# Leaf tiles that gather their rows through a slot-to-token table, in place of rows scattered into block order

## The chip, the cores and the metric

The kernel runs on one core of a Trainium2 chip. A core has a matrix engine (TensorE, PE in the profile), a vector engine (VectorE, DVE), a scalar engine (ScalarE, ACT), GpSimd (POOL) and a sync engine (SyncE, SP) that issues transfers; 16 DMA engines carry them out. SP, ACT and POOL each have a queue from which they issue DMAs; an indirect DMA, whose rows are addressed by a table of indices in on-chip memory, is issued from POOL. The metric is the device time of one execution in microseconds (us); lower is better.

## The reference

The input is x, 4 sequences of 1024 tokens with 256 features. The result is a "macaron": half a feed-forward block, an attention, half a second feed-forward block, each on a layernorm of x:

```python
x = x + 0.5 * ffn(layernorm(x), weights)
x = x + attention(layernorm(x), ...)          # 16 heads, causal by pages of 64
x = x + 0.5 * ffn(layernorm(x), weights)      # the same weights
```

The feed-forward block is itself made of four hard-routed trees (q, k, v and f), each of depth 8 with 256 leaves, and a softmax attention over 256 features between them:

```python
def fff(x, nw, nb, w1, b1, w2, b2, act):
    node = 0
    for _ in range(8):
        node = 2 * node + 1 + (x . nw[node] + nb[node] > 0)
    leaf = node - 255
    return act(x @ w1[leaf] + b1[leaf]) @ w2[leaf] + b2[leaf]   # 256 -> 16 -> 256

xn = normalised x
q, k, v = fff(xn, q...), fff(xn, k...), fff(xn, v...)           # relu
y = xn + softmax(q k^T / 16) v
ffn = y + fff(y, f...)                                           # gelu
```

Every token thus goes to one of 256 leaves in each tree, and each leaf has its own two small weight matrices.

## The kernel before, in words

The 4096 tokens are 32 token tiles of 128 rows (NT). The 256 leaves of a tree are 32 blocks of 8 (NBLK). The top five levels of a tree choose the block; the last three levels are decided inside the block.

**Routing.** `routes` (L392) and `route` (L349) take four token tiles at a time: TensorE transposes rows, multiplies them with the top nodes and with a table of ancestors, and VectorE makes a one-hot of the block for each token (`oh`) and running counts per block (`acc`). For q, k and v one pass serves all three trees.

**Placement.** `place` (L511) gives each token a slot. Blocks come in order, and each block's run of slots is rounded up to whole tiles of 128, so a "leaf tile" holds tokens of one block alone; there are at most 63 leaf tiles (NGRP). `counts`, `tiles_of`, `ends_of` and `ranks` (L423 to L455) compute the slot as the block's first slot plus the token's rank in it, the rank by a product with a triangular matrix; `blocks_ended` and `tile_blocks` (L463, L499) compute which block each leaf tile belongs to (`gblk`, `sel`, `own`).

**Scatter.** `scatter` (L586) sends the normalised rows of one token tile from on-chip memory to a DRAM array `xs` at the slots: one indirect DMA on POOL a token tile, 32 a tree (L593). Slots that no token fills must hold harmless numbers, so the arrays are cleared once at the start (`clear`, L300), two of 8064 KB on SP's queue for q, k and v, and one for f on ACT's queue during the tree attention. In f's array each row has one more column, the token's number, and the padding holds 4096 there.

**Leaves.** `leaves` (L704) works through the leaf tiles in a software pipeline, one iteration a tile: `load` (L709) issues a plain 128 KB load of the tile's rows on SP, four tiles ahead (PRE); `turn` transposes it on TensorE (L718) and ACT evicts it (L720); `hidden` multiplies with the block's 8 first-layer matrices and the 7 lower nodes (L736), and VectorE makes the mask of the leaf taken (L752, L756, L759) and applies it (L766); `active` transposes the masked hidden values (L780) and the mask (L781), ACT applies the activation (L789), VectorE scales the transposed mask (mT, L791); `result` multiplies with the second-layer matrices (L797) and with b2 (L798). For q, k and v ACT evicts the result (L812) and SP stores it in slot order (`osrt`); for f VectorE adds the row (L802) and POOL scatters the rows back to their tokens (`ytok`, L803), leaving out those numbered 4096 or more. Tiles 0 to 47 always run; `spare_leaves` (L685) runs 48-52, 53-57 and 58-62 only where the count of used tiles asks for them.

**Between the trees.** `load_first` (L653) builds the first-layer weights of a tree: 64 transposes and 16 evictions of about 1 us (L675 on VectorE, L677 on ACT). `with_steps` (L1022) interleaves the leaf tiles of q (and of k) with the placement and the scatters of the next tree. During v's leaves, and in the tree attention, `fetch` (L836) gathers the q, k and v results back into token order by the slots (L842, one indirect DMA on POOL a token tile and tree).

**Head of the first block.** After the routing, `split_b2` (L273) loads the four b2, splits them into three bf16 parts (POOL, L288 and L290) and writes the parts by 56 plain DMAs on ACT's queue into DRAM images; then `load_b1` (L628) loads b1 and the lower nodes' offsets by 48 DMAs on ACT's queue and splits them on VectorE. Only then come the placement of q, its 32 scatters, and the rest of the weights' build.

**f.** The tree attention, a token tile a step, is written in program order on TensorE, VectorE, ACT and POOL (`in_order`, L130): what an engine is to do comes in exactly the order of the code. A plan (`at`, `due`) hangs small pieces on its 32 steps. f is routed there as soon as a tile's y is ready (`weigh`, L870), and placed in three runs (`in_runs`, L530), so that the scatters of the first 24 token tiles go out during steps 27 to 29, four more at step 30, and the last four after the last route, between the evictions of the weights' build (L1222-1247). The f leaf stage and the addition to the residual close the block.

## Time and profile before

| what | us |
|---|---|
| three runs, median (lowest to highest) | 2688.52 (2675.3 to 2690.43) |
| the profiled execution, its own time | 2682.69 |
| its span in the trace | 2680.8 |
| TensorE busy | 2214.2 (83%) |
| VectorE busy | 1440.4 (54%) |
| ScalarE busy | 1061.1 (40%) |
| GpSimd busy | 628.3 (23%) |
| first leaf tile turned (L718), first block | 185.4 |
| first leaf tile turned, second block | 1874.6 |
| q leaf stage, tiles 0 to 47, first and second block | 192.7 to 277.1, 1880.7 to 1963.4 |
| f leaf stage, tiles 0 to 47, first and second block | 868.0 to 943.5, 2558.0 to 2635.2 |

In a row of groups the profile gives the line, the engine, the operation, what it writes and reads, how often, its busy time and mean duration, and the idle time of the engine just ahead of it with what ended it. In a list of waits it gives the engine and line that waited, on which engine and line, how long in total, how often, and the longest. A window row gives the window's start and end, its length, and for each engine its busy time and number of instructions, then TensorE's granted clock (1.00 is full speed), the busy share of the DMA engines and their GB/s. The TensorE clock granted over the execution was 0.921.

### The profile page before, as it was taken

The numbers are of one execution on the slowest core, as the hardware profiler recorded it, in microseconds if no ns is written. First come the engines' busy times: TensorE is split into PE (matmuls) and PEld (weight loads), VectorE is DVE, ScalarE is ACT, GpSimd is POOL, SyncE is SP. The second block draws the span as 40 slices with busy tenths as digits, with TensorE's granted clock in tenths as the row PEclk, the third lists the DMA queues.
The fourth block names the chain that finished last, engine by engine and source line by source line (L and its number), as shares of the span: only waits on it lengthen the run. The fifth ranks groups of instructions, "written<-read, shape, count | busy, mean of one in ns | idle before, by whom it ended". The sixth has DMA issues, their size and how long they took to land. (4 is left out here: it accounts for less than half of the span.)

```text
span 2680.8 us, 42431 instructions
## 1 busy us (share of the span) xinstructions
PE 2214.2 (83%) x13989; PEld 1414.2 (53%) x13989; DVE 1440.4 (54%) x4870; ACT 1061.1 (40%) x2645; POOL 628.3 (23%) x752
## 2 busy tenths in 40 slices
PE   5038689899996979999999999972958899999684
PEld 2037568666664854443444434331747776666473
DVE  6046566433343876666666667743646553333375
ACT  4024345422223313555555555551434452222241
POOL 0244042322331621100101100004303222332243
PEclk9569899999998979999999999996989899999897
DMA  8676667423214420000000000015556662320434
GB/s 272 206 278 201 222 197 235 156 61 93 83 46 144 149 70 1 1 1 1 1 1 1 1 1 1 1 61 203 187 202 202 213 182 81 104 91 31 161 122 154
DMA packets 230592, 296.21 MB, mean 110 GB/s; under 512 B 25786, under 2 KB 208715, under 8 KB 226257
## 3 DMA queue, kind: packets, MB, share of 16 engines
q1 hardware_dynamic: 150704, 172.27, 19.7%
q0 software_dynamic: 26352, 67.20, 7.7%
q10 hardware_dynamic: 53296, 53.72, 6.3%
q8 instruction: 130, 2.13, 0.3%
q14 instruction: 110, 0.89, 0.1%
HBM read 165.97 MB, written 131.96 MB: 111 GB/s over the span
## 5 line engine op out<-in xcount | busy, mean ns | idle before, releaser
L1461 DVE TENSOR_REDUCE mxh<-big 128x1 f32<-128x512 f32 (+3 forms) x768 | 393.1, 552 | 193.8 <-PE big L1453 191.8
L1497 ACT ACTIVATE pTh<-big 128x512 f32<-128x512 f32 (+3 forms) x768 | 341.3, 491 | 289.1 <-PE big L1453 265.3
L1453 PE MATMUL big<-kTh,qTh 32*128 32x512 f32 (+3 forms) x1536 | 403.1, 540 | 1.5 <-ACT kTh L1434 1.4
L1489 PE MATMUL big<-qTh,kTh 32*128 32x512 f32 (+3 forms) x1536 | 399.8, 536 | 1.9 <-ACT pTh L1497 1.6
L720 ACT COPY xgT<-sm 128x256 f32<-128x256 f32 x399 | 148.9, 375 | 286.8 <-PE sm L718 141.1
L855 PE MATMUL two<-kT,qT 128*128 128x512 f32 x512 | 239.8, 613 | 10.2 <-issue 8.9
L883 PE MATMUL sm<-vb,pT 128*128 128x256 f32 x1024 | 238.2, 387 | 0.2 <-ACT pT L879 0.2
L1489 PEld LDWEIGHTS big<-qTh,kTh 32*128 32x128 f32 x1536 | 143.3, 184 | 156.7 <-issue 127.0
L718 PE MATMUL sm<-ident,xg 128*128 128x128 f32 x798 | 159.0, 283 | 76.2 <-DMA xg<-xs 73.1
L883 PEld LDWEIGHTS sm<-vb,pT 128*128 128x128 f32 x1024 | 193.8, 194 | 26.9 <-ACT pT L879 1.0
L863 DVE TENSOR_REDUCE mx<-two 128x1 f32<-128x1024 f32 x64 | 78.3, 1223 | 206.0 <-PE two L855 167.6
L1508 PE MATMUL sm<-pTh,vpad 128*32 128x512 f32 (+3 forms) x1536 | 165.4, 502 | 0.0
L1453 PEld LDWEIGHTS big<-kTh,qTh 32*128 32x128 f32 x1536 | 146.9, 185 | 20.4 <-issue 14.3
L855 PEld LDWEIGHTS two<-kT,qT 128*128 128x128 f32 x512 | 96.2, 198 | 111.0 <-issue 107.8
L752 DVE SCALAR_TENSOR_TENSOR went<-sm,sides 128x14 bf16<-128x14 f32 x399 | 66.9, 168 | 152.6 <-PE sm L743 77.5
L780 PE MATMUL sm<-ident,hm 128*128 128x128 f32 x399 | 113.9, 285 | 39.2 <-DVE hm L766 29.0
L812 ACT COPY og<-sm 128x256 f32<-128x256 f32 x298 | 111.1, 373 | 74.5 <-ACT hid L789 30.4
L842 POOL DMA_INDIRECT y_q<-os_q,slot_q x64 | 60.4, 944 | 314.0 <-PE sm L1054 309.8
L718 PEld LDWEIGHTS sm<-ident,xg 128*128 128x128 f32 x798 | 85.7, 148 | 87.0 <-issue 66.5
L789 ACT ACTIVATE hid<-sm 128x128 f32<-128x128 f32 x399 | 112.6, 282 | 45.5 <-PE sm L781 34.1
L803 POOL DMA_INDIRECT ytok<-og,tok x101 | 99.4, 984 | 125.2 <-DVE four L756 94.9
L885 DVE SCALAR_TENSOR_TENSOR xn<-sm,rs,xn 128x256 f32<-128x256 f32 x64 | 31.0, 485 | 170.6 <-PE sm L883 118.7
(316 smaller groups left out, 4279.4 us busy)
## 6 DMA issues: line engine op xcount, KB each, us to landing
xg<-xs SPq DMA_DIRECT2D x298, 128.0 KB
xs<-zero SPq DMA_DIRECT2D x2, 8064.0 KB
xs_f<-zero ACTq DMA_DIRECT2D x14, 1028.0 KB
xg<-xs_f SPq DMA_DIRECT2D x101, 128.5 KB
os_q<-og SPq DMA_DIRECT2D x101, 128.0 KB
os_v<-og SPq DMA_DIRECT2D x101, 128.0 KB
os_k<-og SPq DMA_DIRECT2D x96, 128.0 KB
raw_q<-in_q_w SPq DMA_DIRECT2D x8, 1024.0 KB
```

Of the source, the lines that this page charges most:

```text
L718: nc.tensor.transpose(pa[:, c, :], xg[:, c * P : (c + 1) * P], ident)
L720: nc.scalar.copy(xT, pa)
L780: nc.tensor.transpose(pt[:, 0], hm, ident)
L789: nc.scalar.activation(hid, pt[:, 0], func)
L812: nc.scalar.copy(og, po)
L855: nc.tensor.matmul(ps[:, n0 : n0 + 512], qT[:, c, i * P : (i + 1) * P], kT[:, c, n0 : n0 + 512], start=(c == 0), stop=(c == KC - 1),)
L883: nc.tensor.matmul(po, pT[:, j, :], vb[:, j, :], start=(j == 0), stop=(j == TPB - 1))
L1453: matmul = nc.tensor.matmul(ps[:, :n], qT[r : r + HPAD, hg, i * P : (i + 1) * P], kT[r : r + HPAD, hg, n0 : n0 + n], start=True, stop=True,)
L1461: nc.vector.tensor_reduce(maxima(b, hg)[:, i, c, u : u + 1], ps[:, :n], AX.X, ALU.max)
L1489: matmul = nc.tensor.matmul(ps[:, off:], kT[r : r + HPAD, hg, j * P : (j + 1) * P], qT[r : r + HPAD, hg, qb * QN + off : (qb + 1) * QN], s ...
L1497: nc.scalar.activation(pT[:, u, off:], ps[:, off:], AF.Exp, scale=1.0 / math.sqrt(HD))
L1508: nc.tensor.matmul(acc[r : r + HPAD, off:], vpads[b % 2][:, j, 4 * hg + 2 * pair + u, :], pTs[pair][:, u, off:], start=(j == 0), stop=(j = ...
```

## The change

**No more row arrays in block order.** The scatters of rows, the clearing of their arrays, the extra token column and its cast are gone. In their place the normalised rows are kept in DRAM in token order, with 128 zero rows behind them (`rows`, `keep_rows`): for q, k and v by eight plain stores of 512 KB on ACT's queue during the routing, for f by one store of 128 KB on SP's queue per token tile. `leaves.load` becomes an indirect gather on POOL, whose indices are a column of a table `inv`: for each leaf tile the tokens in its 128 slots, and a number of at least 4096 where there is none. f scatters its results by the same table. The first 48 tiles of a tree also issue the gathers of the four tiles behind them.

**The table.** `placement` replaces `place`, `ranks` and `in_runs`. It takes eight token tiles at a time (for f pieces of 8, 8, 8, 4 and 4). `low` computes each token's rank in its block, how many whole tiles lie before it and its lane in the tile, and a one-hot of the lane. `high` adds the block's first tile and makes a one-hot of the leaf tile, multiplied once by the token tile's base less 4096 and once by the token's own partition number; products of the lane one-hot with these two sum up the table. For f, `low` of the first three pieces is hung on steps 12, 20 and 27, of the fourth on step 31; `low` of the last and all of `high` follow the last route, a step of weights' build between each.

**Other moves.** mT moves from VectorE to ACT. b2's loads go to SP's queue and its writes to POOL's, and `split_b2` is placed ahead of the routing; the loads of b1 go to SP's queue and its splitting from VectorE to POOL. The eight loads of x are issued together at the start. The weights' raw loads have two buffers for q, k and v where they had three.

```diff
-    xs = [dram.tile([NSLOT, E], F32, name=f"xs_{n}") for n in range(2)]
+    rows = [dram.tile([NTOK + P, E], F32, name=f"rows_{n}") for n in "xy"]
     osrt = [dram.tile([NSLOT, E], F32, name=f"os_{nm}") for nm in FFFS[:3]]
-
-    xs += [xs[0], dram.tile([NSLOT, E + 1], F32, name="xs_f")]
     ytok = dram.tile([NTOK, E], F32, name="ytok")
 
 
-    SPARE = (48, 53, 58, NGRP)
-
-
-    zero = const.tile([P, E + 1], F32, name="zero")
-    nc.vector.memset(zero[:, :E], 0.0)
-    nc.vector.tensor_scalar_add(zero[:, E:], pid, float(NTOK))
+    SPARE = (0, 48, 53, 58, NGRP)
+
+
+    zero = const.tile([P, E], F32, name="zero")
+    nc.vector.memset(zero, 0.0)
+    for r in rows:
+        nc.gpsimd.dma_start(r[NTOK:], zero)
...
-            nc.scalar.dma_start(
+            nc.sync.dma_start(
                 rest[f * NBLK : (f + 1) * NBLK].rearrange("p (q c) -> p q c", c=E),
                 a[f"{nm}_b2"].rearrange("(q p) c -> p q c", p=NBLK),
             )
             for lo in (0, B2W - E):
-                nc.scalar.dma_start(b2i[f][:, lo : lo + E], none[:B2R])
+                nc.gpsimd.dma_start(b2i[f][:, lo : lo + E], none[:B2R])
         for s in range(3):
             nc.gpsimd.tensor_copy(part[s], rest)
             if s < 2:
                 nc.gpsimd.tensor_sub(rest, rest, part[s])
-        for f in range(len(FFFS)):
-            for s in range(3):
+            for f in range(len(FFFS)):
                 for r in range(B2G):
                     p = s * NBLK + r * EPB
-                    nc.scalar.dma_start(
+                    nc.gpsimd.dma_start(
...
-    def row_of(f, t):
-        return xn[:, t, : E + (f == 3)]
+    def keep_rows(queue, f, lo, hi):
+        queue.dma_start(
+            rows[f // 3][lo * P : hi * P].rearrange("(i p) e -> p i e", p=P), xn[:, lo:hi, :]
...
+    def placement(pool, oh, acc, pieces, gblk, sel, own, inv, slot=None, ahead=False):
+
+
+
+        parts = {}
+
+        def part(nm, c, shape, dtype, bufs=2):
+            tag = f"{nm}{c}" if ahead else nm
+            return pool.tile(
+                shape, dtype, name=f"{nm}{c}", tag=tag, bufs=1 if ahead else bufs
+            )
+
+        def low(c):
+
+            lo, hi = pieces[c]
+            n, ts_ = hi - lo, slice(lo, hi)
+            pr = sm([P, n, NBLK])
+            nc.tensor.matmul(pr, tri, oh[:, ts_, :], start=True, stop=False)
+            nc.tensor.matmul(pr, ones, acc[:, ts_, :], start=False, stop=True)
+            row = pool.tile([P, n, NBLK], F32, name="row", tag="row")
+            nc.vector.tensor_tensor(row, pr, oh[:, ts_, :], ALU.mult)
             yield
...
+            rank = pool.tile([P, n], F32, name="rank", tag="rank")
+            nc.vector.tensor_reduce(rank, row, AX.X, ALU.add)
+            whole = 1.5 * 2.0**23
+            past = part("past", c, [P, n], F32)
+            nc.vector.tensor_scalar(past, rank, 1.0 / P, 0.5 / P - 0.5, ALU.mult, ALU.add)
+            nc.vector.tensor_scalar_add(past, past, whole)
+            nc.vector.tensor_scalar_add(past, past, -whole)
+            lane = part("lane", c, [P, n], F32)
+            nc.vector.scalar_tensor_tensor(lane, past, -float(P), rank, ALU.mult, ALU.add)
+            yield
+            in_lane = part("in_lane", c, [P, n, P], BF16, 1)
+            nc.vector.tensor_tensor(in_lane, bc(lanes, 1, n), bc(lane, 2, P), ALU.is_equal)
+            parts[c] = past, lane, in_lane
+            yield
+
+        def high(c, first, table):
+
+            lo, hi = pieces[c]
+            n, ts_ = hi - lo, slice(lo, hi)
+            past, lane, in_lane = parts.pop(c)
+            row = pool.tile([P, n, NBLK], F32, name="row", tag="row")
+            nc.vector.tensor_tensor(row, oh[:, ts_, :], bc(first, 1, n), ALU.mult)
+            at = pool.tile([P, n], F32, name="at", tag="at")
+            nc.vector.tensor_reduce(at, row, AX.X, ALU.add)
+            nc.vector.tensor_add(at, at, past)
+            if slot is not None:
+                nc.vector.scalar_tensor_tensor(
+                    slot[:, ts_], at, float(P), lane, ALU.mult, ALU.add
+                )
+            yield
+            tiles = pool.tile([P, n, GCOL], BF16, name="tiles", tag="tiles")
+            nc.vector.tensor_tensor(tiles, bc(numbers, 1, n), bc(at, 2, GCOL), ALU.is_equal)
+            both = pool.tile([P, n, 2, GCOL], BF16, name="both", tag="both", bufs=2 - ahead)
+            nc.scalar.activation(both[:, :, 1], tiles, AF.Copy, scale=pid)
+            yield
+            nc.vector.tensor_tensor(both[:, :, 0], tiles, bc(starts[:, ts_], 2, GCOL), ALU.mult)
+            pi = sm([P, 2, GCOL])
+            for i in range(n):
+                nc.tensor.matmul(
+                    pi, in_lane[:, i, :], both[:, i], start=(i == 0), stop=(i == n - 1)
+                )
+            yield
+            if c:
+                nc.vector.tensor_tensor(table, table, pi[:, 0], ALU.add)
+            else:
+                nc.vector.tensor_scalar_add(table, pi[:, 0], float(NTOK))
+            nc.vector.tensor_tensor(table, table, pi[:, 1], ALU.add)
+            yield
+
+        def rest(done=0):
+
+            ng = tiles_of(pool, counts(pool, acc, NT))
+            yield
+            end = ends_of(pool, "gend", ng, 0.0)
+            first = pool.tile([P, NBLK], F32, name="first", tag="first")
             nc.vector.tensor_sub(first, end, ng)
...
             yield
...
+            table = pool.tile([P, GCOL], F32, name="table", tag="table")
+            for c in range(len(pieces)):
+                if c >= done:
+                    yield from low(c)
+                yield from high(c, first, table)
+            nc.vector.tensor_copy(inv, table)
             found = []
...
+            yield from blocks_ended(pool, acc, found)
             yield
...
+            tile_blocks(pool, found[0], end, gblk, sel, own)
+
+        return low, rest
...
-        nc.vector.memset(b1[:, P + SUB :], 0.0)
+        nc.gpsimd.memset(b1[:, P + SUB :], 0.0)
         yield
-        nc.vector.tensor_copy(b1p[f], b1)
+        nc.gpsimd.tensor_copy(b1p[f], b1)
         for k in range(1, 3):
             for q in range(k, 3):
                 one = slice(q * NBLK, (q + 1) * NBLK)
-                nc.vector.tensor_sub(b1[one], b1[one], b1p[f][one])
-                nc.vector.tensor_copy(b1p[f][one], b1[one])
+                nc.gpsimd.tensor_sub(b1[one], b1[one], b1p[f][one])
+                nc.gpsimd.tensor_copy(b1p[f][one], b1[one])
...
         def load(g):
-            width = xs[f].shape[1]
-            xg = pool.tile([P, width], F32, name="xg", tag="xg", bufs=PRE + 3 * (1 + f // 3))
-            nc.sync.dma_start(xg, xs[f][g * P : (g + 1) * P, :])
+            if g < SPARE[1] + PRE:
+                xg = pool.tile([P, E], F32, name="xg", tag="xg", bufs=PRE + 3 * (1 + f // 3))
+            else:
+                xg = pool.tile([P, E], F32, name="xh", tag="xh", bufs=2 + 4 * (f // 3))
+            nc.gpsimd.indirect_dma_start(
+                out=xg,
+                out_offset=None,
+                in_=rows[f // 3],
+                in_offset=bass.IndirectOffsetOnAxis(ap=inv[:, g : g + 1], axis=0),
+            )
             return xg
...
-            nc.vector.tensor_scalar(mT, pt[:B2R, 1], own[:, g : g + 1], None, ALU.mult)
+            nc.scalar.activation(mT, pt[:B2R, 1], AF.Copy, scale=own[:, g : g + 1])
...
-                tok, xg = kept.pop(g)
-                nc.vector.tensor_tensor(og, po, xg[:, :E], ALU.add)
+                nc.vector.tensor_tensor(og, po, kept.pop(g), ALU.add)
                 nc.gpsimd.indirect_dma_start(
                     out=places[g],
-                    out_offset=bass.IndirectOffsetOnAxis(ap=tok, axis=0),
+                    out_offset=bass.IndirectOffsetOnAxis(ap=inv[:, g : g + 1], axis=0),
...
+        end = hi if part else hi + PRE
         for g in range(lo - PRE, hi + 5):
-            if g + PRE < hi:
-                rows[g + PRE] = load(g + PRE)
+            if g + PRE < end and g + PRE not in got:
+                got[g + PRE] = load(g + PRE)
...
+        keep_rows(nc.sync, 3, t, t + 1)
...
+                        if first:
+                            for t in range(0, NT, GT):
+                                nc.sync.dma_start(
+                                    xres[:, t : t + GT, :],
+                                    a["x"][
+                                        t // TPB, (t % TPB) * P : (t % TPB + GT) * P, :
+                                    ].rearrange("(i p) e -> p i e", p=P),
+                                )
+                            split_b2(stage(rt, "b2", 1))
...
+                            keep_rows(nc.scalar, 0, lo, lo + GT)
...
-                    drain(placing(0, None, slot[0]))
-                    drain(scattering(0, slot[0], None, NT))
-                    drain(build)
+                    drain(placing(0), build)
...
-                        ahead = load_raw(raw, f + 1, 3)
-                        rows = []
-                        with_steps(
-                            leaves(*what),
-                            placing(f + 1, rows),
-                            scattering(f + 1, slot[f + 1], rows, 1),
-                        )
+                        ahead = load_raw(raw, f + 1)
+                        with_steps(leaves(*what), placing(f + 1))
...
+                pieces = [(0, 8), (8, 16), (16, 24), (24, 28), (28, 32)]
+                low_f, rest_f = placement(
+                    pf, *hot_f, pieces, gblk[3], sel[3], own[3], inv[3], ahead=True
+                )
+                paths, lows = [], {}
...
+                for c, step in ((0, 12), (1, 20), (2, 27)):
+                    for i in range(3):
+                        at(step + i // 2, 1 + i % 2, place_low, c)
                 for where in range(3):
-                    at(31, where, place_run, 1, 1)
+                    at(31, where, place_low, 3)
...
-                    place_run(2, 1)
-                    drain(islice(build, 3))
-                    place_run(2, 1)
-                    go(*range(RUNS[2], NT))
-                    for _ in range(3):
-                        place_run(2, 1)
-                        drain(islice(build, 2))
+                    place_low(4)
+                    drain(islice(build, 2))
+                    place_low(4)
+                    place_low(4)
+                    for _ in rest_f(len(pieces)):
+                        drain(islice(build, 1))
                     drain(build)
```

## The prediction

> **What bounds the kernel now.** I read the page's totals first, then the windows by stage, the chain of waits, the groups of GpSimd (POOL), and last the timelines of the leaf stages.
>
> ```profile
> span 2680.8 us, 42431 instructions
> PE 2214.2 (83%) x13989; PEld 1414.2 (53%) x13989; DVE 1440.4 (54%) x4870; ACT 1061.1 (40%) x2645; POOL 628.3 (23%) x752
> ```
>
> TensorE bounds the whole, but 17% of the span is holes, and the change touches only these and the leaf stages. Windows (busy us and counts of PE, PEld, DVE, ACT, POOL; granted clock; DMA):
>
> ```profile
> 75.00:100.00 25.00, 2.03 (x6) 0.56 (x6) 0.46 (x3) 0.00 (x0) 3.30 (x2) 0.50 0.85 277
> 100.00:125.00 25.00, 0.00 (x0) 0.00 (x0) 0.00 (x0) 0.00 (x0) 11.28 (x7) 0.50 0.45 133
> 150.00:175.00 25.00, 3.65 (x16) 3.27 (x16) 4.24 (x4) 4.08 (x4) 18.90 (x21) 0.56 1.04 390
> 192.00:277.00 85.00, 75.73 (x561) 63.37 (x560) 57.71 (x284) 41.78 (x138) 30.66 (x32) 0.99 0.62 202
> 422.00:497.00 75.00, 73.70 (x596) 65.47 (x595) 52.98 (x233) 48.08 (x159) 19.84 (x21) 1.00 0.64 188
> 868.00:944.00 76.00, 72.18 (x545) 60.89 (x546) 68.01 (x324) 26.10 (x92) 44.35 (x46) 1.00 0.44 135
> 1830.00:1870.00 40.00, 4.83 (x41) 4.48 (x39) 6.50 (x7) 6.04 (x6) 25.96 (x28) 0.62 0.76 277
> ```
>
> Two heads are nearly empty: 75 to 185 us, and 1830 to 1870 us. The leaf stages of q (192-277), v (422-497) and f (868-944) each do 48 leaf tiles with TensorE 89 to 98% busy; in f VectorE is at 89% too. POOL has room everywhere: 0.26 to 0.58 of a stage. The waits name the first head:
>
> ```profile
> POOL b_part L288 <- DMA b2i_f<-b_none: 94.6, 1, 94.6
> DVE cnt L428 <- DMA b_f<-in_f_nb: 59.7, 1, 59.7
> PE sm L718 <- DMA xg<-xs: 73.1, 4, 37.9
> DVE xn L885 <- remote: 40.7, 6, 9.0
> ```
>
> The routing is done by 70 us; b2 then waits for its loads behind the clearing of the row arrays (2 x 8064 KB), and the split (97-111) and the writes of b2 and b1 on ScalarE's queue last until 133. Slots come at 141, 32 scatters run until 182, and the first leaf tile is turned (L718) at 185.4. The POOL groups (busy, mean ns | idle before):
>
> ```profile
> L593 POOL DMA_INDIRECT xs<-xn,slot_q x64 | 61.7, 964 | 85.7 <-DVE slot_q L454 66.8 <-issue 18.0 <-DMA xs<-xn,slot_q 0.6
> L842 POOL DMA_INDIRECT y_q<-os_q,slot_q x64 | 60.4, 944 | 314.0 <-PE sm L1054 309.8 <-issue 4.3
> L803 POOL DMA_INDIRECT ytok<-og,tok x101 | 99.4, 984 | 125.2 <-DVE four L756 94.9 <-DVE went L752 17.7 <-issue 6.2
> ```
>
> An indirect DMA costs POOL 0.94 to 0.98 us, scatter or gather, plus a gap. The timelines show the gap and a side effect (start, duration, [idle before <- releaser]):
>
> ```profile
> 535.69 0.95 POOL L842 DMA_INDIRECT vb<-os_v,slot_v  x1 [0.30 <-issue]
> 543.36 1.22 DVE L863 TENSOR_REDUCE mx<-two 128x1 f32<-128x1024 f32 x1 [9.54 <-remote]
> 228.62 0.96 POOL L593 DMA_INDIRECT xs<-xn,slot_k  x1 [0.30 <-issue]
> 229.95 0.96 POOL L593 DMA_INDIRECT xs<-xn,slot_k  x1 [0.36 <-issue]
> 231.70 0.37 ACT L720 COPY xgT<-sm 128x256 f32<-128x256 f32 x1 [1.88 <-PE sm L718]
> 873.51 0.98 POOL L803 DMA_INDIRECT ytok<-og,tok  x1 [0.55 <-DVE four L756]
> ```
>
> Back to back, one gather takes 1.25 us (0.95 + 0.30). After 17 such gathers (519-540) VectorE had stood for 9.5 us for a matmul long finished: completions of TensorE reach the others late while POOL issues without pause. In the q stage every third tile stalls 1.3 us after three scatters in a row (tile intervals 1.51, 1.51, 2.81). In f, one scatter per 1.54 us leaves gaps of 0.55 and nothing stalls. So a leaf stage is as fast as TensorE only while POOL pauses.
>
> **The change part by part**, against the profiled execution's own 2682.7 us (span 2680.8), which lies 5.8 below the median of 2688.5.
>
> **First head.** Clears and 32 scatters leave; b2 starts at once. POOL: loads in by about 25 us (5 MB of x and b2 at 246 GB/s, the first window's rate, from 3 us), three casts and two subtractions 3 x 1.89 + 2 x 4.05 = 14 us, 58 plain DMAs (8 `none`, 48 parts, 2 zero tails), then b1's copies, moved from VectorE, some 8 us. No row shows a plain DMA of POOL: ScalarE's queue took 0.35 to 0.9 us each for the same writes, an indirect one of POOL takes 1.25; I take 1.25 as the row of the same engine, 73 us. End: 25+14+73+8 = 120; the first gather (1.25) and its landing (2.1) give 123. The other end (0.35 each, 20 us) makes POOL free at 67; then the placement ends it: routing 70, four pieces of 5.3 us of VectorE (five 256-element operations at 0.42 us, one of 1024 at 1.2 and two of 512 at 0.68, as L863 and L879 have them, and four small ones at 0.15) with a hop through ScalarE and TensorE, about 30, so 104. First turn 123 for 185.4: **-62** (-81 to -45; the 48 b1 loads, now on SP's queue ahead of the weights, hide beside the routing). What is late next is w1: its 16 evictions of 1.06 us follow the placement in order, and L736 needs them two tiles after the turn.
>
> **Second head.** Slots at 1819.5-1826 and scatters until 1868 become a placement of about 29 us from 1819.5, then a gather: first turn 1857 for 1874.6, **-18** (-30 to -10).
>
> **q and k stages.** Scatters of the next tree, with their stalls, leave (1.78 to 1.58 us a tile, 47 intervals: -9.4), and 48 gathers spread at one per tile come: 0.95 of 1.58 us, so a pause of 0.63, as f has now. mT leaves VectorE (L791, 340 ns) for ScalarE, whose three evictions (375+282+373 = 1.03 us) become 1.3 of 1.55, hidden. The placement of the next tree (21 us of VectorE, 36 small matmuls of TensorE, 3 us) replaces ranks and 32 slot casts. **-9 x 4 = -36** (-44 to -16). Each of the four starts of k and v makes two to three gathers (1.25) ahead of its first tile, behind the spares: **+12** in all.
>
> **v stages.** POOL has 52 gathers and 24 fetches (L842) in each: 76 x 1.25 = 95 us for 75-77. Bare, +14 to +18 each; with no pause, late completions add a few: **+40** (+28 to +60). The fetches can't be hidden elsewhere: the gather of a tile is queued behind them in program order.
>
> **f stages.** Now each tile has a gather and a scatter on POOL: 1.25 + (0.98 + 0.30) = 2.53 us for 1.59. The scatter waits for og, and the gathers of four tiles on are queued behind that wait; `hidden` waits for them. VectorE loses mT and the cast (0.48 of 1.42 us a tile) for nothing. Bare: 0.94 x 47 = +44. With POOL never pausing, the q row (1.3 us per three DMAs in a row) gives at worst 0.8 us a tile more, 3.3; I take 2.8, since a scatter that waits is itself a pause: **+57 each** (+44 to +81). The Trainium skill ("DMA: Bandwidth & Descriptors", Issuing engines are not separate DMA queues) says that the choice of issuing engine only saves "the time on the sequencer it takes to initiate the DMA, which is usually small relative to the DMA itself"; by it moving the loads costs nothing, f stays at 1.6, and the sum below falls by 150. Here the initiation is the row: SP's issue of xg has a median of 383 ns, POOL's 1250, and the consumer's period is 1.59. I go by the row.
> Around f: the table needs all routes, then one `low` and five `high` steps, some 25 us of VectorE with their hops, between w1 evictions in strict program order, with ScalarE behind its own weight-load issue (831-849 before), in place of slot casts and the last four scatters (11 us, ended at 842): **+14 each** (0 to 21). The scatter bursts in the tree attention (9 us of `remote` waits at 784-794) leave: **-8 each**; the tail gets a shorter chain, **-5 each**. The stores of rows there are 32 plain stores on SP, idle there: 0 (-2 to +5).
>
> **Spares.** Four of their gathers issued ahead save a landing and an issue, some 3 us (2.1 + 1.25), in each of three taken parts: **-10** (-15 to +3).
>
> Sum: -62 - 18 - 36 + 12 + 40 + 2 x (57 + 14 - 8 - 5) - 10 = **+42**: 2725 of the profiled 2683, hence **2730** against the median.
>
> **The rivals.**
> Bare queue: POOL is the limit at 2.53 in f and v at the bare +28, but completions are not late. Sum: -62 - 18 - 36 + 12 + 28 + 2 x (44+14-13) - 10 = +4: 2692. For: gathers write SBUF in pieces and waits break POOL up. Against: the 9.5 us above came from gathers.
> The head pays more than booked: the mechanism is DMA and POOL freed in the first 100 us. If plain POOL DMAs cost 0.35 us and the pieces of placement overlap so that the first turn is at 88 (18 us after the routing), the head gives -97, and with bare f the sum is 4 - 35 = -31, with spares and q, k at their good ends -45: **2645**. It decides from a first turn before about 95 us with f at no more than 2.53. For: all engines idle at 75-130. Against: the serial table chain.
> Stalls in full: f at 3.3, v at its upper end: +42 + 48 + 20 = +110: 2798.
> That the table saves no scatter is excluded: L593 is removed.
>
> **How the numbers follow.** Forecast 0.42, bare queue 0.17, the head 0.22, full stalls 0.19. About 1% (27 us) is what a measurement of this kernel can tell from no change. Forecast and full stalls are slower, bare is same: faster 0.22, same 0.17, slower 0.61. The range reaches from the head's good case to near the full stalls, 2640 to 2800; slower alone 2705 to 2800.
>
> **What would show it.** First turn at 105-125 for 185; POOL without 0.5 us gaps in f, hidden's tile interval 2.5-3.3 there; q and k tile intervals without the 2.81; v stage at 90-105 us; waits of L718 on xg gathers. The prediction is wrong if gathers in f are issued closer than 1.25 us, or if the b2 DMAs on POOL delay x or the routing.

## The result, and the profile after

The change makes the kernel slower. On the same chip the kernel before took 2686.3 us (median) and the changed kernel 2793.9 us (2793.2 to 2797.3): ratio 1.041, 95% interval 1.0376 to 1.0443, so +107.5 us where +42 had been summed. The profiled execution took 2793.3 us, its span 2791.5, 110.7 more than before.

The page's totals of the changed kernel:

```profile
span 2791.5 us, 43145 instructions
PE 2300.0 (82%) x14253; PEld 1477.1 (53%) x14253; DVE 1434.1 (51%) x4458; ACT 1175.0 (42%) x3078; POOL 846.0 (30%) x1005
```

TensorE's busy time rose by 86 us, POOL's by 218, and VectorE's stayed. Windows of the changed kernel by stage (busy us and counts of PE, PEld, DVE, ACT, POOL; granted clock; DMA): first head, q and k leaf stages, v, f.

```profile
75.00:100.00 25.00, 2.90 (x20) 1.98 (x20) 14.37 (x49) 1.44 (x2) 12.60 (x36) 0.50 0.60 192
100.00:125.00 25.00, 10.27 (x63) 9.26 (x64) 12.57 (x34) 6.42 (x7) 6.74 (x7) 0.64 0.39 112
135.00:223.00 88.00, 78.75 (x596) 66.47 (x596) 57.06 (x258) 55.99 (x192) 47.27 (x46) 0.96 0.69 196
255.00:339.00 84.00, 77.43 (x598) 64.78 (x597) 56.66 (x257) 55.78 (x192) 43.23 (x42) 1.00 0.56 142
373.00:473.00 100.00, 77.73 (x596) 65.79 (x596) 39.20 (x185) 56.27 (x207) 60.75 (x64) 0.99 0.52 143
842.00:977.00 135.00, 97.58 (x542) 76.53 (x543) 57.69 (x229) 38.18 (x137) 87.26 (x87) 0.79 0.25 72
```

The dead head is 57 us shorter: q's stage starts at 135 for 193. But v lasts 100 us for 75, with TensorE's work the same within 4 us, and f 135 for 76. In f the granted clock falls from 1.00 to 0.79, and TensorE is busy for 98 us with the work that took 72. The POOL timeline of f (start, duration, [idle before <- releaser]):

```profile
892.81 1.02 POOL L758 DMA_INDIRECT ytok<-og,inv_f  x1 [0.30 <-issue]
894.13 0.97 POOL L665 DMA_INDIRECT xg<-rows_y,inv_f  x1 [0.30 <-issue]
895.41 1.02 POOL L758 DMA_INDIRECT ytok<-og,inv_f  x1 [0.30 <-issue]
896.73 0.98 POOL L665 DMA_INDIRECT xg<-rows_y,inv_f  x1 [0.30 <-issue]
...
905.22 1.02 POOL L758 DMA_INDIRECT ytok<-og,inv_f  x1 [1.34 <-DVE four L714]
```

Scatter and gather alternate with gaps of 0.30 us, 2.6 us a tile, broken now and then by a wait of over a microsecond for a result. Such a hold-up in v, in the timeline of several engines:

```profile
422.74 0.38 PE L676 MATMUL sm<-ident,xg 128*128 128x128 f32 x2
422.89 0.95 POOL L798 DMA_INDIRECT y_q<-os_q,slot_q  x1 [0.30 <-issue]
...
424.65 0.17 DVE L710 SCALAR_TENSOR_TENSOR went<-sm,sides 128x14 bf16<-128x14 f32 x1 [2.65 <-PE sm L676]
424.75 0.37 ACT L678 COPY xgT<-sm 128x256 f32<-128x256 f32 x1 [1.92 <-PE sm L676]
```

The transposes of 422.7 had ended by 423.1; ScalarE takes them at 424.75, 1.6 us later, after POOL's third indirect DMA in a row had ended at 423.8.

Stage by stage (a leaf stage is counted from the start of ScalarE's activation of tile 0 to that of tile 47, both blocks together, us; the second head is the stretch from f's tile 47 of the first block to q's tile 0 of the second):

| term | expected | measured |
|---|---|---|
| first head | -62 | -57.2 |
| second head | -18 | -10.4 |
| q and k stages, four | -36 | +4.6 (334.7 to 339.3) |
| starts of k and v, four | +12 | +11.7 |
| v stages, two | +40 | +51.3 |
| f stages, two | +114 | +117.4 |
| around f (attention, start, tail) | +2 | +1.5 |
| spare tiles | -10 | -8.2 |
| sum | +42 | +110.7 |

The runs below fell in groups of two kinds. In one kind the kernel before takes 2681 to 2693 us, and its two traces have 160 and 178 us of waits with the releaser "remote", that is, waits whose end the profile puts down to no instruction of the core. The longest one stands in this row of the kernel before's list of waits:

```profile
ACT w_q L677 <- remote: 40.3, 5, 15.7
```

There were 24 such waits of over 1.5 us in that trace. In each, VectorE or ScalarE was about to read a result of TensorE, TensorE's last instruction had ended 1.6 to 32 us before, and POOL was issuing indirect DMAs. They are read here as completions of TensorE that arrive late. In the other kind the kernel before takes 2590 to 2594 us, and no kernel's trace has any such wait. They are called the late and the prompt kind, and numbers are compared within a kind unless the text says otherwise. What sets the kind isn't known; that it belongs to the chip isn't shown, since the record gives the same chip number, 8, to a group of each.

### The profile page after: what moved, and what is told of

Its sections match the earlier page's. It is cut to its first block, busy times and chain, and to the rows that moved or that the text cites. A ratio compares the mean times of both kernels' runs of the same rounds, so it can differ in the third digit from the quotient of the medians.

```text
span 2791.5 us, 43145 instructions
## 1 busy us (share of the span) xinstructions
PE 2300.0 (82%) x14253; PEld 1477.1 (53%) x14253; DVE 1434.1 (51%) x4458; ACT 1175.0 (42%) x3078; POOL 846.0 (30%) x1005
## 3 DMA queue, kind: packets, MB, share of 16 engines
q1 hardware_dynamic: 89696, 113.04, 11.7%
## 5 line engine op out<-in xcount | busy, mean ns | idle before, releaser
L1388 DVE TENSOR_REDUCE mxh<-big 128x1 f32<-128x512 f32 (+3 forms) x768 | 393.0, 552 | 193.1 <-PE big L1380 191.1
L736 PE MATMUL sm<-ident,hm 128*128 128x128 f32 x399 | 121.0, 303 | 110.2 <-DVE hm L724 22.6
L665 POOL DMA_INDIRECT xg<-rows_x,inv_q x104 | 107.0, 1029 | 175.1 <-DVE endc L445 62.1
L665 POOL DMA_INDIRECT xg<-rows_x,inv_k x104 | 106.8, 1027 | 111.2 <-PE sm L737 49.3
L665 POOL DMA_INDIRECT xg<-rows_y,inv_f x104 | 101.7, 978 | 108.8 <-PE sm L443 76.0
L736 PEld LDWEIGHTS sm<-ident,hm 128*128 128x128 f32 x399 | 59.0, 148 | 141.4 <-ACT mT L747 37.2
```

Source lines behind the costliest of these rows:

```text
L665: nc.gpsimd.indirect_dma_start(out=xg, out_offset=None, in_=rows[f // 3], in_offset=bass.IndirectOffsetOnAxis(ap=inv[:, g : g + 1], axis=0),)
L736: nc.tensor.transpose(pt[:, 0], hm, ident)
L1388: nc.vector.tensor_reduce(maxima(b, hg)[:, i, c, u : u + 1], ps[:, :n], AX.X, ALU.max)
```

## The experiments

**1. Loads of v and f without the table** (prompt kind).

```diff
+            if f >= 2:
+                n = g % NT * P
+                nc.sync.dma_start(xg, rows[f // 3][n : n + P, :])
+                return xg
```

> The changed kernel, but the leaf tiles of v and f load 128 rows in token order with a plain load on SP's queue, without the table (so v and f work on the wrong rows; the work per tile is the same). Theory: v and f are paced by POOL's indirect DMAs; with the gathers gone POOL has one indirect DMA a tile or less, v (tiles 0 to 47) falls from 100 to 73-78 us, f from 135 to 72-79 us in each block, in all about -165 us, to some 2630. Rival: v and f are slow because mT sits on ScalarE, or because of the reading by the table elsewhere; then both stay within 5 us of 100 and 135, and the time at about 2790.

Measured 2553.5 us (the expected total was reckoned on the times of the late kind). v took 75.7 and 75.2 us, f 70.6 and 70.4. The full changed kernel on the prompt kind (experiment 8) takes 78.6 and 80.7 in v and 113.7 twice in f. So f's loss is the gathers on POOL and nothing else of the change. v's loss was 25 us a stage in the first profile; on the prompt kind it is 4 to 7 (78.6 and 80.7 for 74.5 and 74.2 in the kernel before, by experiment 4).

**2. No placement beside q and k** (prompt kind).

```diff
-                        with_steps(leaves(*what), placing(f + 1))
+                        drain(leaves(*what))
```

> The changed kernel, but no placement runs beside the leaf tiles of q and k: k and v use q's table, slots and blocks (so they work on the wrong rows). Theory: in the q and k stages the placement of the next tree (VectorE 21 us, products on TensorE and a copy on ScalarE in chains) costs about 0.25 us a tile over its 30 tiles; without it the interval of two tiles falls to 1.51-1.56 throughout and a stage gives back 7 to 9 us, four stages 28 to 36 us. Rival: the gathers themselves, by late completions of TensorE, hold the stages; then they stay at 82 to 87 us and the intervals keep their pattern.

Measured 2612.6 us. q took 78.5 and 79.6 us, k 73.9 and 76.7: in all 308.6. With the placement, in run 1 on the same kind, they took 88.0, 86.6, 82.9 and 82.8, in all 340.2. The placement costs 31.6 us. The windows of q and k of both, first without the placement, then with it:

```profile
133.00:212.00 79.00, 73.12 (x555) 63.70 (x554) 41.33 (x187) 51.48 (x187) 46.83 (x46) 0.96 0.71 199
245.00:319.00 74.00, 71.22 (x552) 62.40 (x552) 40.90 (x185) 51.46 (x187) 42.13 (x42) 0.99 0.64 167
```

```profile
133.00:221.50 88.50, 77.15 (x597) 65.80 (x595) 57.06 (x258) 55.59 (x190) 47.64 (x46) 0.96 0.70 203
255.00:338.00 83.00, 76.93 (x596) 64.87 (x594) 56.12 (x254) 55.32 (x190) 43.86 (x42) 0.99 0.56 143
```

TensorE gets 42 to 44 instructions and 4 to 6 us more, VectorE 15.5 us more, in stages where TensorE was busy 93 to 96% without them.

**3. b2 ahead alone, on the kernel before** (prompt kind).

```diff
+                            split_b2(stage(rt, "b2", 1))
-                        with ExitStack() as b2:
-                            split_b2(stage(b2, "b2", 1))
```

> The kernel before with one part of the change alone: b2 split ahead of the routing (b2 and b1 loads on SP's queue, their writes and splitting on POOL, x loaded first, two raw buffers), rows still scattered, arrays still cleared. Theory: of the 57 us that the first head gained, most is b2: slots come at 75 to 100 where they came at 141, 32 scatters take 40 us, the first tile's activation comes at 130 to 150 for 192.7; nothing else moves: 2686 - 45 to - 60 = 2626 to 2641. Rival: the head's gain came from the scatters and clears that went; then b2 ahead gives at most 15 us (2670 or more).

Measured 2593.7 us, ratio 1.0006 (0.9995 to 1.0017): neither was right. The first activation came at 174.7 for 193.1, a gain of 18. q's 32 scatters now started at 102.7 but lasted until 164: b1's pieces stood between them in POOL's order and waited there, 16 us in all, for scatters to land. And q's first stage (80.1 for 74.6) and the four starts of k and v, with two raw buffers in place of three (10 us in all), gave 16 of the 18 back.

**4. One more gather a tile in f, on the kernel before** (prompt kind, and again on the late kind).

```diff
             nc.sync.dma_start(xg, xs[f][g * P : (g + 1) * P, :])
+            if f == 3:
+                fetch(pool, 0, 0, slot_q[0], tag="more", bufs=2)
```

> The kernel before with one more indirect gather of 128 rows on POOL at the load of every leaf tile of f, into a buffer that nobody reads; everything else of f as before (mT on VectorE, no table). Theory: the second indirect DMA a tile alone makes f's tile interval 2.5 to 3.0 us (stage 120 to 140 us for 75.5 and 77.2), total 2686 + 90 to + 125. Rival: the wait for the gathered rows, the table or ScalarE's extra operation make f slow in the changed kernel; then f here stays at 1.6 to 2.0 us a tile, total below 2725.

> The kernel before with one extra indirect gather a leaf tile of f once more, on the chip of this group. It stood at 2.37 us a tile on the chip where no completion came late. Theory: where completions come late while POOL issues without pause, the same kernel takes 2.7 to 3.0 us a tile, as the changed kernel's f does (2.85 to 2.91); without late completions 2.37 again. Rival: the excess of the changed kernel's f over 2.5 comes from its table or its order of work; then 2.4 to 2.5 here on any chip.

Prompt: 2674.9 us for 2593.7, f at 2.37 and 2.35 us a tile; the changed kernel's f there is 2.42. Late: 2806.9 us for 2692.8, f at 2.91 and 2.84; the changed kernel's f there is 2.85 to 2.88. One indirect DMA more on POOL, with no table, no new order and mT where it was, makes nearly the whole of f's loss. Top of the waits in f's first window on the late kind (time, times, longest):

```profile
ACT xgT L722 <- remote: 42.6, 8, 6.2
POOL ytok L805 <- DVE four L758: 33.8, 13, 7.7
```

and on the prompt kind:

```profile
ACT xgT L722 <- PE sm L720: 47.5, 43, 2.3
...
DVE og L804 <- DMA ytok<-og,tok: 23.6, 21, 2.4
```

Few long waits in the first, up to 6.2 us; in the second many short ones, with VectorE's og held by buffers that POOL's scatters have not yet emptied. The granted clock in these windows was 0.80 on the late kind and 0.97 on the prompt kind.

**5. A memset of POOL in place of that gather** (late kind).

```diff
+                more = pool.tile([P, 1024], F32, name="more", tag="more", bufs=1)
+                nc.gpsimd.memset(more, 0.0)
```

> The kernel before with one memset of 128 x 1024 numbers (0.9 to 1.0 us) on POOL at the load of every leaf tile of f, where the earlier run had one more indirect gather (f at 2.37 to 2.38 us a tile). Theory: what counts is POOL's time in its queue, 0.95 + 0.98 and their gaps: f at 1.9 to 2.3 us a tile, stage 90 to 108 us, total 30 to 65 us over the kernel before. Rival: what makes the second gather dear is the DMA (its rows' traffic, its landing, completions held up); then the memset is hidden but for 0.1 to 0.3 us a tile: f at or below 1.75, total within 15 us of the kernel before.

Measured 2718.4 us for 2680.9; f at 2.00 us a tile in both blocks, 94 us a stage, as the theory had it. No wait with the releaser "remote" falls into f's window:

```profile
868.00:962.00 94.00, 75.70 (x546) 60.52 (x545) 68.72 (x322) 28.10 (x92) 81.02 (x83) 1.00 0.37 109
```

POOL is as busy here (81 us) as with the gather (83 us in 137), in 43 us less, and the granted clock stays at 1.00. POOL's queue is full in both: memset and scatter repeat every 2.12 us in mid-stage, gather and scatter every 2.60 on the prompt kind, the 0.97 or 0.98 us of each being much the same and the gaps not (0.17 us in all for 0.60). So f's tile grows in two steps: from 1.6 to 2.0 us with the memset and to 2.4 with the gather by POOL's time in its queue, gaps included (neither f stage has a late completion, so the two kinds are set side by side here), and from 2.4 to 2.9 only on the late kind, with the indirect DMA. In this second step late completions and the lower clock come together; the clock's own part wasn't taken apart.

**6. The changed kernel with f as before, then with fewer fetches in v** (late kind). The first puts f's three runs, row array, scatters and plain loads back; the second also takes eight of the 24 fetches of v's stage into the tree attention.

```diff
-                    for f, b, dst in ((1, 0, kTs), (0, 0, qTs), (1, 1, kTs)):
+                    for f, b, dst in ((1, 0, kTs), (0, 0, qTs)):
```

> The changed kernel with one part undone: f's placement in three runs, its row array, scatters and plain loads as before; q, k and v gather by the table; mT stays on ScalarE. Theory: f's leaf stage falls from 135 to 73-80 us in each block, with all else as in the changed kernel: where the kernel before takes 2681, 2793 - 2 x 58 = 2670 to 2685, ratio to the kernel before 0.995 to 1.003; on a chip without late completions 0.98 to 0.99. Rival: the table of f, issued late, and not f's second indirect DMA holds f; then the scatters in the tree attention take back what f gains and the time stays above 2720.

> As the run before, and v's leaf stage fetches 16 tiles of q and k where it fetched 24, one in three leaf tiles; the other eight (k of the second sequence) are fetched in the first steps of the tree attention. Theory: v's POOL queue falls from 76 to 68 indirect DMAs, with at most one fetch in three gathers; v from 100 to 85-90 us in each block, the tree attention 0 to 5 us longer: 15 to 30 us under the run before, so 0.985 to 0.995 of the kernel before. Rival: v is held by its gathers alone; then v stays above 96 us and the time within 5 us of the run before.

The first: 2689.3 us for 2692.8, ratio 0.9977 (0.9961 to 0.9992); f 83.1 and 84.2 us. f's part of the change costs over 100 us, and the rest about nothing. f stayed 7 us above the kernel before and above the theory's 73 to 80; mT, on ScalarE here, is the difference left in its leaf tiles. The second: 2691.9 us, ratio 0.9992 (0.9976 to 1.0008). v fell to 92.4 and 93.8 from 100.2 and 102.5, less than the 85 to 90 expected, and what lies between v's and f's first block grew from 365.8 to 377.7: the gain was given back by the tree attention.

**7. q alone by the table** (late kind): k and v scattered and loaded as before, 20 of k's scatters written behind q's leaf tiles.

```diff
-                            with_steps(leaves(*what), placing(f + 1, rows), move)
+                            with_steps(leaves(*what), placing(f + 1, rows), few(move, 12))
+                        drain(move)
```

> The parts of the change that paid, without those that cost: b2 ahead of the routing, q alone gathers through the table; k, v and f are scattered and loaded as before (20 of k's 32 scatters after q's leaf tiles), mT on ScalarE in f only. Theory: the first head gives 50 to 60 us, the second 8 to 12, f 3 to 5 in each block, q's stage loses 5 to 10 in each: 45 to 70 us under the kernel before on the same chip. Rival: q's gathers with k's scatters crowd POOL between q and k so that k starts 15 to 30 us later, twice: then within 15 us of the kernel before.

Measured 2718.8 us, ratio 1.0141 (1.0114 to 1.0168); the rival, and more. q's stage took 118.1 and 124.2 us. The POOL groups of q's window:

```profile
L839 POOL DMA_INDIRECT xg<-rows_x,inv_q x38 | 36.7, 964 | 24.6 <-PE sm L875 6.8 <-issue 5.6 <-PE sm L850 4.6
L715 POOL DMA_INDIRECT xs<-xn,slot_k x32 | 31.8, 992 | 18.8 <-issue 5.8 <-DVE slot_k L712 4.9 <-DVE went L884 2.6
```

All 32 scatters of k were scheduled into q's stage, between q's gathers, not behind them. The start gave less too (160 for 193): ahead of q's first gather, at 120.8, POOL waited 24.9 us for the loads of v's b1.

**8. The changed kernel again, on both kinds.**

> The changed kernel itself, beside the kernel before on the same chip. In the second group of runs the kernel before took 2593.7 us where it had taken 2686.3, and its trace showed no late completions of TensorE (no wait with the releaser 'remote', 160 us of them in the first trace). Theory: the loss of the change is made of POOL's issue rate in v and f, of the placement beside q and k, and of late completions while POOL issues without pause; on a chip without late completions f's tile interval is 2.42 (as in the run without the placement) and v's 1.7, the ratio to the kernel before stays above 1.02 and at or below 1.041. Rival: the loss is in late completions alone; then the ratio is within 1% of 1 there.

> The kernel before itself, for a trace beside the other kernels of this group. If this chip is like the second one: no 'remote' waits, q and k stages at 74 to 77 us for 82 to 85, tree attention (last tile of v to the first of f) at about 337 us for 357, first leaf tile still at about 190. If it is like the first one: as in the first trace within 1%.

> The changed kernel once more. Where the kernel before takes about 2590 us (no late completions): the sum of the parts measured on such a chip, q and k +40 (300 to 340), v +5 each, f +44 each, first head -58, second -6, gives 2590 + 74 = 2665, ratio 1.02 to 1.032; late completions alone (rival) would give a ratio below 1.01. Where it takes about 2685: 1.041 again.

Late: 2792.8 us for 2680.9, ratio 1.0415 (1.0386 to 1.0444); the kernel before repeated its first trace (q and k 84.0, 83.9, 83.3, 84.6, first activation 192.7). Prompt: 2676.0 us for 2592.7, ratio 1.0332 (1.0293 to 1.0371). Late completions alone are excluded as the cause of the loss. The parts there, against run 4's q, k, v and head and the last run's f: head -58, q and k +40 (300.1 to 340.0), v +11, f +81 (73.1 and 73.6 to 113.7 each): +74 of the +83.

**9. No placement once more, on the late kind; and no gathers in q and k with the placement kept** (prompt kind).

```diff
+            if f < 2:
+                n = g % NT * P
+                nc.sync.dma_start(xg, rows[0][n : n + P, :])
+                return xg
```

> The changed kernel without the placement beside q and k once more (k and v on q's table, so on the wrong rows), on the chip of this group. Theory where completions come late: q and k lose the placement's 6 to 9 us each and stand at 75 to 80 us; f stays at 2.8 to 2.95 us a tile and v near 2.1, since neither has a placement beside it. Where they don't: q and k at 74 to 79, f at 2.42, v at 1.7, as in the first run of this kernel. Rival: the placement in k's stage is not what costs; then q and k stay above 82.

> The changed kernel, but the leaf tiles of q and k load 128 rows in token order by plain loads on SP's queue (so on the wrong rows), with the placement of the next tree kept beside them. With the placement left out and the gathers kept, q took 78 to 83 us and k 74 to 79. Theory: of q's and k's 84-87 us the placement is 5 to 8 and the gathers, by late completions and the burst at the start, another 4 to 8: here 77 to 81 us. Rival: placement alone; then 83 to 86, as in the changed kernel.

On the late kind, without the placement: q 82.6 and 82.7, k 79.1 and 77.6, in all 322.0, 17 us less than the 339.3 with it (20 less than in experiment 8's repeat); v (101.6) and f (135.2) unchanged. The placement's price there is some 60% of that on the prompt kind; why is open. Without gathers, on the prompt kind: q 85.8 and 86.8, its rival, and k 79.0 and 79.4, within the theory; 9 us less in all than run 1. What is left over the 300.1 of the kernel before, 31 us, has the size of the placement's price in experiment 2.

**10. mT back on VectorE, f as before** (prompt kind).

```diff
-            nc.scalar.activation(mT, pt[:B2R, 1], AF.Copy, scale=own[:, g : g + 1])
+            nc.vector.tensor_scalar(mT, pt[:B2R, 1], own[:, g : g + 1], None, ALU.mult)
```

> As the run with f as before, and mT back on VectorE in all four trees. There f took 83-84 us where the kernel before takes 75-77, and q and k stayed at 83-87. Theory: on ScalarE mT cost f 7 us in each block and q and k nothing; with it back f stands at 74-78, q and k as they were: 12 to 16 us less, ratio to the kernel before 0.990 to 0.994. Rival: mT on ScalarE is also what holds q and k (1.3 us of ScalarE a tile); then q and k fall to 76-80 too, and the ratio to 0.985 or less.

It fell in a group of the other kind than the run that it was to be held against: 2596.2 us for 2590.5, ratio 1.002 (1.0007 to 1.0033). q and k took 89.2, 85.6, 89.5 and 87.5 us, longer than with mT on ScalarE (88.0, 82.9, 86.6, 82.8): mT on ScalarE isn't what holds them, it helps. f took 73.7 and 73.4; with mT on ScalarE and no gathers (run 1) 70.6 and 70.4. On the late kind it is the other way round: in experiment 7 mT is on ScalarE in f alone, and f took 79.8 and 80.8 us for 74.9 and 77.2 in the kernel before of the same group. So some 4 of the 7 us of experiment 6 go with mT there; the rest stays open.

**11. b2 ahead with one clear moved** (prompt kind): as in experiment 3, the second 8064 KB clear behind q's weights, three raw buffers in the second block.

```diff
-                            tc.keep_in_program_order(clear(nc.sync, xs[1]))
+                        tc.keep_in_program_order(clear(nc.sync, xs[1]))
```

> The kernel before with b2 ahead, as in the run of that part alone, but the second clear of a row array (8064 KB) moved behind q's weights, and three raw buffers kept in the second block. Theory: in the run of b2 alone its b1 loads and q's scatters waited behind 16 MB of clears (first activation at 174.7), and two raw buffers cost 3 us ahead of each of k and v; here the first activation comes at 140 to 155 for 193, the second block is as before: 30 to 50 us under the kernel before, ratio 0.981 to 0.989. Rival: the clear only moves into q's stage, where it holds q's loads and k's scatters as long; then ratio 0.995 to 1.005.

Measured 2567.3 us for 2592.7, ratio 0.990 (0.9868 to 0.9932): faster than both kernels, by 25 us where the theory had 30 to 50. The first activation came at 152.3, 41 us earlier, as expected; q's first stage, beside which the clear now runs, took 78.7 for 74.6. It was not run on the late kind. Its windows from 75 to 150 us:

```profile
75.00:100.00 25.00, 6.70 (x35) 6.25 (x35) 10.26 (x32) 4.25 (x4) 15.82 (x24) 0.57 1.04 343
100.00:125.00 25.00, 1.19 (x6) 1.22 (x7) 0.00 (x0) 0.07 (x1) 19.19 (x21) 0.50 0.78 254
125.00:150.00 25.00, 8.42 (x42) 7.04 (x41) 6.09 (x16) 5.25 (x7) 5.07 (x15) 0.57 0.96 338
```

POOL's 32 scatters run from 84.6 to 125.1 us without a break, and b1's pieces of v and f, which stood between them in experiment 3, come behind them; what still stands empty is mostly the time of these scatters.

## Why the prediction was right or wrong

**First head: near in number, in part by luck.** It gave -57 by the first activation, -54 by the first turn, for -62. The first gather went out at 110.4 us, between the ends of 104 and 123: POOL's plain DMAs took 0.50 us each (b2i writes, eight in 4 us), nearer the lower end than the 1.25 taken. With the landing of 2.1 us that the prediction took, that alone would have turned the first tile at about 114. But w1, which was to be late two tiles after the turn, lay ahead of the first turn in TensorE's order: its transposes waited twice for raw loads, 7.0 us in all, so that the first tile was turned at 131. **Second head: -10 for -18**: the table took 27 us, near the 29 expected, but the 19 us of w1's build followed it where they had been hidden under the scatters. The **starts of k and v** fit their +12 by luck: those of v took 9.0 and 7.1 us more, those of k 3.9 and 0.5 less.

**f: held in mechanism and size.** +59 a stage for +57, with 2.88 and 2.87 us a tile for the 2.8 taken. On the prompt kind it lost 40 a stage, near the bare 44. By the rows, POOL's price of an indirect DMA and its gap decided, and the sentence of the Trainium skill ("DMA: Bandwidth & Descriptors", Issuing engines are not separate DMA queues), by which the sequencer's time is "usually small relative to the DMA itself", did not apply: experiment 4 shows the loss with that one instruction a tile. **v: +51 for +40**, the causes right (fetches and gathers in one queue, completions late), their shares not. v's window holds 64 indirect DMAs, not 76, and 64 x 1.25 is 80 us: that is what v takes on the prompt kind, a loss of 5 a stage where the bare queue had been put at 14 to 18. Most of the 25 on the late kind is therefore what that kind adds, late completions after three DMAs in a row by the rows above, which the sum had put at "a few".

**q and k: the step that failed.** "VectorE 21 us, 36 small matmuls of TensorE, 3 us" was set beside other work and booked at nothing, and the scatters' stalls were booked as -9 a stage: -36 in four stages, where +4.6 was measured. The interval of about 3 us at every third tile, which runs through half of q's and k's stages in the kernel before, did go. But the placement took its place. Its rows in k's window of the changed kernel:

```profile
L499 DVE TENSOR_TENSOR in_lane<-lanes,lane 128x1024 bf16<-128x1024 bf16 x4 | 4.9, 1217 | 0.0
L519 DVE TENSOR_TENSOR tiles<-numbers,at 128x512 bf16<-128x512 bf16 x4 | 2.7, 685 | 0.0
L526 PE MATMUL sm<-both,in_lane 128*128 128x128 bf16 x32 | 2.4, 219 | 0.0
```

By its lines the placement was 23.8 us of VectorE and 9.4 us of TensorE's instruction time in that stage, for 9.5 and 1.5 in the kernel before (overlaps of pipelined products counted in full). The VectorE time had been estimated well, TensorE's somewhat low; what was wrong was to book them at nothing. Without the placement a stage was 8 us shorter on the prompt kind, 4 to 5 on the late kind. TensorE is busy 89 to 92% of these stages, so its added products have little room, and a VectorE operation of 1.22 us stands ahead of the next tile's mask; which of the two costs how much is argued, not shown, since the placement was only taken out whole.

On the late kind, for which the sum was made, the placement is 17 of the 40.6 us missed: the sum had the four stages at 299, they took 322.0 without the placement and 339.3 with it. The other 23 sit mostly in the first tiles. Without the placement the first four intervals of the four stages sum to 46 us, where sixteen tiles at the forecast 1.58 would be 25. In q they sum to 13.0 and 12.9 us in the changed kernel, for 7.8 and 7.6 in the kernel before; they are about 13 without the placement too, and 13.7 and 14.6 with plain loads (experiment 9, prompt kind). TensorE waits there for q's second-layer weights. The wait, both blocks together, in the changed kernel and then without the placement on the late kind:

```profile
PE sm L753 <- DMA w_q<-in_q_w: 5.1, 2, 3.0
```

```profile
PE sm L753 <- DMA w_q<-in_q_w: 10.4, 2, 5.3
```

No q or k stage of the kernel before has such a wait. The load of these weights (4096 KB) goes out on SP's queue behind q's raw weights: 12 us ahead of the first turn in the changed kernel (119.3 for 131.1), 39 in the kernel before (146.2 for 185.4). The prediction named w1 as late next, not this load: part of what the heads gained was paid back in q's stage. In the later tiles, from the fifth to the thirtieth interval, beside which the placement runs, a tile took 1.82 us on average in both kernels. Without the placement it took 1.61 on the late kind and 1.52 on the prompt kind, where 1.58 had been forecast.

On the prompt kind, where the stalls hardly exist (300.1 for the kernel before), 32 of the 40 us are the placement's. That the other 8 are the gathers' is not shown: without the placement the tiles after the start took 1.52 us with the gathers in place, and TensorE waited 13 us for the second-layer weights of q and k.

The miss of 69 us is thus 41 in q and k, 11 in v, 12 in the heads, 3 in f and 2 in the spare tiles. The rival of full stalls gave a time near the measured one, 2798, for the wrong reason: f's pace of 3.3 didn't come; it was the gain that failed to come.

## What to carry to other kernels

A transfer moved to an indirect DMA costs its issue time on GpSimd for every tile: compare that, gap included, with the consumer's period on that queue together with all else in it, before counting what the move saves elsewhere. Work put "beside" a stage is hidden only on engines that have room in that stage; price the added instructions on the engine that paces it first. And try the parts of a change apart: here one part (b2 ahead, with a clear moved out of its way) was the better kernel, by 1.0% on the prompt kind.

## What the runs showed of the hardware

The same kernel before ran in 2681-2693 us in some groups and in 2590-2594 in others, about 3.5% apart, and the profile shows a difference: in the slower ones VectorE and ScalarE waited up to 15.7 us at a time for results of TensorE while POOL issued indirect DMAs back to back. With one extra indirect gather a tile in f the same code ran at 2.91 us a tile in one kind and 2.37 in the other, with a granted clock of 0.80 and 0.97; with a memset of the same length, on the late kind, at 2.00 and without such waits, at a clock of 1.00. What makes a completion late was not found, nor what sets the kind. The ratio of the change differed with it (1.041 and 1.033), and so did the list of what it cost: v +51 on one, +11 on the other; q and k +5 and +40.

An indirect DMA of 128 rows holds POOL 0.94 to 1.02 us and is followed by a gap of 0.30 us when the next is an indirect DMA too; a plain DMA of b2 on POOL took 0.50 us.
